# Taking four blocks' second 128 columns as they lie, in a sparse graph kernel with row gathers

## The chip, the cores and the metric

The kernel runs on one core of one Trainium2 chip. The time is the device time in microseconds (us) of one execution; for the kernel before it is 993.78 us, the median of 3 runs (992.75 to 998.94). The trace that is read below comes from one further execution under the hardware profiler, which took longer than the timed ones (the table below has it).

The engines are named as in the profile: PE is TensorE's matmul, PEld its weight load, DVE VectorE, ACT ScalarE, POOL GpSimd and SP SyncE, which here only issues DMAs.

## The reference: four graph layers over one sparse matrix

`x` is 2708 x 512, `adj` is 2708 x 2708 with 24,436 entries that aren't zero; they are dense in the low rows and columns and on the diagonal. Each layer adds something to `x` and normalizes the rows:

```python
# layer 0: degree-normalized sum, then a product with W
adj_hat = adj + eye;  d = 1 / sqrt(adj_hat.sum(1))
x = layernorm(x + (d[:, None] * adj_hat * d[None, :]) @ x @ W.T + b)
# layer 1: every positive entry raised by its row's share, divided by the degree
head = (adj > 0) / max(norm of the row, eps);  inc = adj + head
x = layernorm(x + (inc @ x) / inc.sum(1))
# layer 2: attention weights e on the entries; h = x @ W_sa
s = s_left[:, None] + s_right[None, :]
e = where(adj != 0, exp(-leaky_relu(s, 0.01)), 0);  x_a = (e / e.sum(1)) @ h
x_b = adj @ (x @ W_gcnb) + b_gcnb
x = layernorm(x + sigmoid(gate_a * x_a + gate_b * x_b))   # gates from adj @ x and x
# layer 3: product of signs, summed over the neighbours
x = layernorm(x + relu(adj @ (max(sign(x), 0) @ sign(weight).T)))
```

## The kernel before

The 2708 rows are 22 blocks of 128 (the last has 20). For one block of rows only some columns of `adj` hold anything. The kernel finds them on the chip and packs them: a *tile* is 128 such columns (as rows of `adj_t`, 128 x 128 in SBUF, in `packed[b]`), and the rows of the features that belong to them are fetched by an indirect DMA, a *gather* of 128 rows whose addresses stand in `index[b]`. A block's sum is then a chain of matmuls, one per tile, into one PSUM bank. The packed tiles and the indices are made once and used by all four layers.

`ROOM[b]` is how many gathered tiles block `b` has. `DIRECT[b]` names column blocks that are not searched: they are taken as they lie, 128 x 128 of `adj_t` by a plain DMA on SP's queue (line 1000), and their features are a block already in SBUF, so that they need no gather. Before, only block 1 has more than column block 0. Block 0 itself takes all 22 column blocks directly. `HALVES[b]` is (tiles whose columns only reach the upper 64 rows of the block, tiles for the lower 64 rows); a half tile has 64 columns of weights, and an upper and a lower one can share the PE array. `in_turns` sets the order: whole tiles, direct ones first, then upper and lower in turns.

The stages:

- *Search and layer 0's product* (lines 678 to 1268). SP streams `adj` row block by row block in the order of `arrival` (block 0 last). `mark` (line 806) clears the direct columns' part of a mask (line 845) and counts hits by matmuls; `count`, `steps_of`, `look_up` (ACT copies the table, line 931) and `list_nodes` (line 966) turn them into indices, for the groups of blocks in `GROUPS` at once. `list_nodes` also issues the direct tiles' loads. `fetch` (line 1012) then gathers the group's packed tiles from `adj_t` on POOL. After every second of these gathers POOL writes zeros into a scratch tile nobody reads (line 1020), but only for the groups in `RESTED`: all but the last three, that is up to blocks 12 to 14. In between, `y = x @ W` of each block is made, scaled and stored to DRAM (`y_rows`). The instructions of this stage are kept in the written order on each engine (`in_order`).
- *Layer 0* (from line 1319) takes the blocks in the order 1, 21, 2, 3, ..., 20. `gathered` (line 582) gathers rows of `y_rows` on POOL into a ring of 10 tiles. The positive entries are counted for layer 1, and block 0's layer 1 sum grows block by block (`grow1`).
- *Layer 1* (from line 1513) gathers from `x1_rows` into a ring of 8, makes its weights on DVE in runs of up to three tiles of one kind (lines 1601, 1602), and projects each finished block for layer 2 (line 1537).
- *Layer 2* (from line 1629) gathers rows of x and h together (1026 columns) into a ring of 7 (line 1725), makes the attention weights in parts of up to three tiles on ACT and DVE, and multiplies each tile twice (line 1748).
- *Layer 3* (from line 1916) gathers 16-bit rows of `xw_rows` for blocks 21 and 5 to 20, while the sums of blocks 0 to 4 run over all columns (`whole_tile`). Halves aren't used here.

A gather runs on POOL, in order with everything else there; its data land later through the DMA engines. If the found columns don't fit `ROOM` and `HALVES`, a flag (`over`) starts a dense version of the whole computation behind the sparse one.

Of the kernel before, what the change touches and what calls it, by code (L numbers as in the profile page):

```python
# [27 lines left out]

ROOM = (0, 8, 8, 7, 6, 6, 6, 5, 5, 5, 5, 4, 5, 4, 4, 4, 4, 4, 4, 4, 3, 1)


DIRECT = {1: (0, 1), 2: (0,), 3: (0,), 4: (0,), 5: (0,), 7: (0,), 8: (0,), 9: (0,), 11: (0,),
          13: (0,), 14: (0,), 15: (0,), 16: (0,), 17: (0,), 20: (0,)}

HALVES = ((0, 0), (3, 3), (3, 3), (2, 3), (2, 2), (2, 3), (2, 2), (2, 2), (2, 2), (2, 2), (2, 2),
          (1, 1), (2, 2), (1, 1), (1, 1), (1, 2), (1, 2), (1, 2), (1, 1), (1, 2), (1, 1), (0, 0))  # L40
HALF = 64

GROUPS = (
# [452 lines left out]
def sparse_layers(ctx, tc, x, adj, adj_t, w0_t, b0, w_sa, a_sa, w_gcnb, b_gcnb, wa, ba, wb, bb, w3_t,  # L496
# [33 lines left out]

    f = [feat.tile([P, D], F32, tag=f"f{b}", name=f"f{b}") for b in range(NB)]
    f0_other = feat.tile([P, D], F32, tag="f0_other", name="f0_other")
    first = [f[0], f0_other]
    packed = [feat.tile([P, NB, P], F32, tag="a0", name="a0")] + [
        feat.tile([P, tiles(b), rows(b)], F32, tag=f"a{b}", name=f"a{b}") for b in range(1, NB)
    ]
# [39 lines left out]
    head0_row = const.tile([P, P], F32, name="s_head0_row")  # L576
    cols = const.tile([P, NB, EXTRA], F32, name="s_cols")

    def own_by_itself(b: int) -> bool:
# [89 lines left out]
    with tc.tile_pool(name="s_pre", bufs=1) as pre:  # L669
# [10 lines left out]
        row_sums = pre.tile([P, NB, 2], F32, name="s_row_sums")  # L680

        def place_of_x(b: int):
            return f[b] if b else first[1]

        def load(b: int):
            m = rows(b)
# [119 lines left out]
        def mark(b: int, others):  # L806

            others = iter(others)  # L810

            def other():
                next(others, lambda: None)()

            g = group_of[b]
            i = g.index(b)
            m = rows(b)
            if i == 0:
                find = ps_s.tile([P, D], F32, tag="find", name=f"find{b}", bufs=2)
                n = len(g)  # L820
                search[g] = {
                    "hits": find[:, : n * NB * 3].rearrange("p (g s c) -> p g s c", g=n, c=3),
                    "before": find[:, n * NB * 3 : n * (NB * 3 + 3)],
                    "diff": find[:, D - n * NT * 4 :],
                }
            mask = masks[arrival.index(b) % 2]
            for ar, c0 in zip(arows[b], (0, CUT)):
                nc.vector.tensor_scalar(
                    mask[:m, c0 : c0 + ar.shape[1]], ar, 0.0, None, op0=ALU.not_equal
                )  # L830
                other()
                own = b * P - c0
                if own_by_itself(b) and 0 <= own < ar.shape[1]:
                    nc.vector.scalar_tensor_tensor(
                        mask[:m, b * P : b * P + m], ar[:, own : own + m], 0.0, off_dia[:m, :m],
                        op0=ALU.not_equal, op1=ALU.mult,
                    )
                    other()
                    scr = small.tile([P, P], F32, tag="dia", name=f"dia{b}", bufs=1)
                    nc.vector.scalar_tensor_tensor(  # L840
                        scr[:m, :m], ar[:, own : own + m], 1.0, ident[:m, :m],
                        op0=ALU.mult, op1=ALU.mult, accum_out=dia[:m, b : b + 1],
                    )
            for j in direct(b):
                nc.vector.memset(mask[:m, j * P : (j + 1) * P], 0.0)
            for step_ in others:
                step_()
            for s in range(NB):
                nc.tensor.matmul(
                    search[g]["hits"][:, i, s, :], mask[:m, s * P : (s + 1) * P], sides[:m],  # L850
                    start=True, stop=True,
                )
# [152 lines left out]
                at += ROOM[b]  # L1005

        to_fetch = []
        RESTED = GROUPS[:-3]
        fetched = [0]
        rest = pre.tile([P, 384], F32, name="s_rest")  # L1010

# [102 lines left out]
        def head_steps(g):  # L1114
# [41 lines left out]

            def keep_heads():
                hr = counts_of.pop(g)
                dst = head0_row if g == (0,) else head_row[:, b0_ * P : b0_ * P + G * m]
                nc.scalar.copy(dst, hr[:, : G * m])  # L1160

            return [counts, roots, shares, spread, keep_heads]

        counts0 = small.tile([P, 2], F32, tag="counts", name="counts0", bufs=1)

        def count_block0():
# [111 lines left out]
    bw = wp.tile([P, KC, D], BF16, name="s_bw")  # L1278
    sequence = [0, 1, NB - 1, *range(2, NB - 1)]

    def features(b: int, i: int, old0):

        j = direct(b)[i]
        return f[j] if j else old0


    def span(b: int, i: int):
# [39 lines left out]
    with tc.tile_pool(name="s_l0", bufs=10, reuse_waits="tile") as lp:  # L1327


        a_row = lp.tile([P, 2, D], F32, tag="a_row", name="s_a_row", bufs=1)  # L1330
        vec = lp.tile([P, 2, KC], F32, tag="vec", name="s_vec", bufs=1)
        b0_row = lp.tile([P, D], F32, tag="b0_row", name="s_b0_row", bufs=1)
        nc.scalar.dma_start(b0_row, over_partitions(b0, D))

# [31 lines left out]
        def grow1(j: int):  # L1366

            r = rows(j)
            inc = lp.tile([P, P], F32, tag="inc0", name=f"inc0_{j}", bufs=2)
            a = packed[0][:r, j, :]  # L1370
            nc.vector.scalar_tensor_tensor(
                inc[:r], a, 0.0, head0_row[:r], op0=ALU.is_gt, op1=ALU.mult
            )
            nc.vector.tensor_tensor(inc[:r], inc[:r], a, op=ALU.add)
            nc.tensor.matmul(  # L1375
                sum1, inc[:r], (f[j] if j else first[1])[:r, :D], start=(not grown1),
                stop=(len(grown1) == NB - 1),
            )
            grown1.append(j)
# [17 lines left out]
        for n, g in enumerate(GROUPS):  # L1397
            steps_ = head_steps(g)
            between.setdefault(2 + 2 * n, []).append(
                several(lambda g=g: count_positive(g, lp), steps_[0])  # L1400
            )
            between.setdefault(3 + 2 * n, []).append(several(*steps_[1:]))
        for at, b in enumerate(sequence):
            m = rows(b)
            old = place_of_x(b)
            nc.vector.tensor_tensor(old[:m, :D], old[:m, :D], b0_row[:m], op=ALU.add)
            if b:
                nd = len(direct(b))
                order_ = in_turns(b)
                src = {}  # L1410
                for i in order_:
                    if i >= nd:
                        src[i] = gathered(lp, D, y_rows, b, i - nd)
                    elif direct(b)[i] == b:
                        src[i] = lp.tile([P, D], F32, tag="own", name=f"y_own{b}", bufs=1)
                        nc.sync.dma_start(src[i][:m], y_rows[b * P : b * P + m, :])
                    else:
                        src[i] = first[0]
                ps = ps_mm.tile([P, D], F32, tag="mm", name=f"l0_{b}")
                for i in order_:  # L1420
# [12 lines left out]
            for step_ in between.get(at, []):  # L1433
                step_()
# [27 lines left out]
    state = {}  # L1462

    def old_new(b: int):
        return (f[b], f[b]) if b else (first[0], first[1])

    def open_block(b: int, pool, ps_pool, tag: str):

# [30 lines left out]

    def finish1(b: int, ps):  # L1500
        m = rows(b)
        old, new = (f[b], f[b]) if b else (first[1], first[0])
        t = work.tile([P, D], F32, tag="t", name=f"t1_{b}")
        nc.scalar.activation(t[:m], old[:m, :D], AF.Copy, scale=own1[:m, b : b + 1])
        nc.vector.scalar_tensor_tensor(
# [5 lines left out]
    with tc.tile_pool(name="s_l1", bufs=8, reuse_waits="tile") as lp:  # L1511
# [407 lines left out]
    with tc.tile_pool(name="s_l3", bufs=11, reuse_waits="tile") as lp, \  # L1919
# [13 lines left out]

        turn = [0]

        def widened(t, r: int, name: str):

            g = lp.tile([P, D], F32R, tag="wide", name=f"w{name}", bufs=4)
            turn[0] += 1
            if turn[0] % 3 == 0:  # L1940
                nc.vector.tensor_copy(g[:r], t[:r])
# [6 lines left out]
        def finish3(b: int, ps, more: bool):  # L1948

            m = rows(b)  # L1950
            old = f[b] if b else first[1]
# [35 lines left out]

        whole = [ps_w.tile([P, D], F32, tag=f"w{b}", name=f"l3_{b}") for b in range(WHOLE3)]

        def whole_tile(j: int):  # L1990
# [21 lines left out]
        for at, b in enumerate(order3):  # L2012
# [121 lines left out]
```

## Time and profile before

| What | us |
|---|---|
| median of 3 runs (lowest, highest) | 993.78 (992.75, 998.94) |
| the profiled execution | 1049.87 |
| its span, first to last instruction | 1048.1 |
| PE busy | 884.9 |
| DVE busy | 660.3 |
| POOL busy | 524.8 |
| first gather of layer 0 | 199.0 |
| first gather of layer 1 | 368.8 |
| first gather of layer 2 | 602.8 |
| first matmul group of layer 3 | about 917 |

In the lines of the profile, "L1014" is a line of the kernel, "out<-in" are the names of tiles, and "x12" is a count. Times in the timeline and in the chain of waits count from the span's start. In a timeline the first number is the start, the second how long the instruction (or the merged row of instructions) took, and the bracket at the end is how long the engine stood idle before it and what ended that: "issue" and "remote" or "another core or an unknown queue" mean that the profile sees nothing that ended it. DMA_INDIRECT is a gather[...].

### The profile page before, as it was taken

The numbers are of one execution on the slowest core, as the hardware profiler recorded it, in microseconds if no ns is written. First come the engines' busy times: TensorE is split into PE (matmuls) and PEld (weight loads), VectorE is DVE, ScalarE is ACT, GpSimd is POOL, SyncE is SP. The second block draws the span as 40 slices with busy tenths as digits, with TensorE's granted clock in tenths as the row PEclk, the third lists the DMA queues.
The fourth block names the chain that finished last, engine by engine and source line by source line (L and its number), as shares of the span: only waits on it lengthen the run. The fifth ranks groups of instructions, "written<-read, shape, count | busy, mean of one in ns | idle before, by whom it ended". The sixth has DMA issues, their size and how long they took to land.

```text
span 1048.1 us, 13071 instructions
## 1 busy us (share of the span) xinstructions
PE 884.9 (84%) x3759; PEld 467.4 (45%) x3777; DVE 660.3 (63%) x2598; ACT 385.7 (37%) x824; POOL 524.8 (50%) x555
## 2 busy tenths in 40 slices
PE   1999885567879959999999989988788999689993
PEld 1545442122223224545555533444444555467862
DVE  4889795545657745554654456666577777655675
ACT  3665562000000114534444433333333333255553
POOL 1688885766766254644532053343243333066761
PEclk9999997778989988999999999999899999889996
DMA  9999982667767454766554266776566665299985
GB/s 285 345 348 329 314 279 62 204 177 213 221 207 214 144 177 142 220 187 188 178 176 129 102 229 217 260 243 203 173 223 208 202 192 181 80 280 315 328 240 174
DMA packets 94759, 225.07 MB, mean 215 GB/s; under 512 B 13900, under 2 KB 28092, under 8 KB 94676
## 3 DMA queue, kind: packets, MB, share of 16 engines
q0 software_dynamic: 44784, 132.86, 42.7%
q1 hardware_dynamic: 37944, 76.51, 21.3%
q10 hardware_dynamic: 11948, 14.76, 4.4%
q8 instruction: 32, 0.52, 0.2%
q14 instruction: 51, 0.42, 0.1%
HBM read 182.80 MB, written 31.71 MB: 205 GB/s over the span
## 4 chain that ended last, share of the span: by engine, by line
PE 58%; DVE 12%; DMA 12%; issue 6%; another core or an unknown queue 4%; ACT 4%; POOL 3%; ACTq 0%; POOLq 0%; DVEq 0%; SPq 0%
PE l L1320 16%; DMA xg<-x_rows,i 9%; PE h L1537 7%; PE l L2003 5%; PE a L1748 4%; PE e L1748 4%; PE l L2042 3%; PE pg L1800 3%; PE y L1048 2%; PE pc L1800 2%; POOL a L1014 2%; PE l L1375 2%; PE e L1570 2%; PE a L1571 1%
## 5 line engine op out<-in xcount | busy, mean ns | idle before, releaser
L1725 POOL DMA_INDIRECT xg<-x_rows,i x102 | 100.3, 984 | 180.3 <-PE e L1748 45.2
L584 POOL DMA_INDIRECT xg<-x_rows,i x102 | 98.0, 961 | 117.5 <-PE l L1320 74.2
L1014 POOL DMA_INDIRECT a<-in_adj_t_dram,row_at x102 | 112.2, 1100 | 61.9 <-DVE deg L773 26.5
L584 POOL DMA_INDIRECT xg<-y_rows,i x102 | 103.1, 1010 | 48.3 <-issue 23.5
L1320 PE MATMUL l<-xg,a 128*64 128x512 f32 (+2 forms) x204 | 91.4, 684 | 12.4 <-DMA xg<-y_rows,i 12.4
L1748 PE MATMUL a<-xg,a 128*64 128x512 f32 (+2 forms) x204 | 91.4, 602 | 4.7 <-DMA xg<-x_rows,i 4.7
L584 POOL DMA_INDIRECT xg<-xw_rows,i x73 | 74.3, 1018 | 40.8 <-issue 18.6
L1748 PE MATMUL e<-xg,ae 128*64 128x512 f32 (+2 forms) x204 | 89.3, 602 | 1.4 <-ACT ae L1498 1.4
L1048 PE MATMUL y<-s_w,xt 128*128 128x512 f32 (+1 forms) x176 | 87.4, 642 | 1.6 <-issue 0.9
L1537 PE MATMUL h<-s_wsa,xt 128*128 128x256 f32 (+3 forms) x352 | 83.8, 392 | 3.0 <-issue 1.9
L1537 PEld LDWEIGHTS h<-s_wsa,xt 128*128 128x128 f32 (+1 forms) x352 | 65.7, 190 | 29.0 <-issue 10.7
L1320 PE MATMUL l<-xg,inc 128*64 128x512 f32 (+2 forms) x204 | 73.4, 609 | 2.5 <-DMA xg<-x_rows,i 2.3
L1493 ACT ACTIVATE ae<-sl,xg 128x64 f32<-128x64 f32 (+2 forms) x102 | 35.8, 359 | 84.8 <-DMA xg<-x_rows,i 76.0
L765 ACT ACTIVATE unused<-arow 128x1408 uint8<-128x1408 f32 (+3 forms) x44 | 58.3, 1325 | 3.6 <-DMA x_rows<-s_zero 2.0
L613 ACT ACTIVATE rsqs<-mv 128x1 f32<-128x1 f32 (+2 forms) x56 | 11.3, 202 | 126.2 <-DVE mv L642 42.8
L2003 PE MATMUL l<-ws,pw 128*128 128x512 f32 (+1 forms) x210 | 51.3, 398 | 4.8 <-DVE pw L1931 4.8
L1800 PE MATMUL pg<-s_wg,pt 128*128 128x256 f32 (+1 forms) x176 | 46.0, 403 | 8.2 <-ACT pt L1788 8.2
L1048 PEld LDWEIGHTS y<-s_w,xt 128*128 128x128 f32 (+1 forms) x176 | 33.2, 199 | 39.6 <-issue 38.0
L1494 DVE SCALAR_TENSOR_TENSOR ae<-ae 128x128 f32<-128x128 f32 (+4 forms) x60 | 19.9, 334 | 47.8 <-ACT ae L1493 41.9
L1544 DVE COPY h<-h 128x260 f32<-128x260 f32 (+1 forms) x20 | 8.6, 428 | 64.9 <-PE h L1537 41.6
L1320 PEld LDWEIGHTS l<-xg,a 128*64 128x64 f32 (+2 forms) x204 | 23.7, 167 | 55.9 <-issue 51.8
L2003 PEld LDWEIGHTS l<-ws,pw 128*128 128x128 f32 (+1 forms) x210 | 39.7, 190 | 14.8 <-DVE pw L1931 5.6
(302 smaller groups left out, 1854.0 us busy)
## 6 DMA issues: line engine op xcount, KB each, us to landing
arow<-in_adj_dram SPq DMA_DIRECT2D x21, 704.0 KB
arow<-in_adj_dram SPq DMA_DIRECT2D x21, 650.0 KB
x_rows<-f SPq DMA_DIRECT2D x41, 256.0 KB
aw<-in_adj_t_dram SPq DMA_DIRECT2D x21, 320.0 KB
f<-in_x_dram SPq DMA_DIRECT2D x20, 256.0 KB
y_rows<-yt ACTq DMA_DIRECT2D x20, 256.0 KB
out_dram<-f SPq DMA_DIRECT2D x20, 256.0 KB
x_rows<-h SPq DMA_DIRECT2D x19, 257.0 KB
```

Source lines behind the costliest of these rows:

```text
L584: nc.gpsimd.indirect_dma_start(out=t, out_offset=None, in_=src[:, :], in_offset=bass.IndirectOffsetOnAxis(ap=index[b][:, i : i + 1], axis=0),)
L765: nc.scalar.activation(unused[:m, : ar.shape[1]], ar, AF.Copy, accum_out=row_sums[:m, b, h : h + 1])
L1014: nc.gpsimd.indirect_dma_start(out=packed[b][:, t + len(direct(b)), :], out_offset=None, in_=adj_t, in_offset=bass.IndirectOffsetOnAxis(ap ...
L1048: nc.tensor.matmul(ps[:m], xt[:, k, :m], w0[:, k, :], start=(k == 0), stop=(k == KC - 1))
L1320: nc.tensor.matmul(ps[r0:r1], weights, moving, start=(i == order[0]), stop=all(span(b, j) != (r0, r1) for j in order[order.index(i) + 1 :] ...
L1493: nc.scalar.activation(ev[:, i, :], sl, AF.Identity, bias=score)
L1537: nc.tensor.matmul(ps, xt[:, k, :m], w[:, k, :], start=(k == 0), stop=(k == KC - 1))
L1725: nc.gpsimd.indirect_dma_start(out=g, out_offset=None, in_=x2_rows[:, :], in_offset=bass.IndirectOffsetOnAxis(ap=index[b][:, t : t + 1], a ...
L1748: nc.tensor.matmul(ps[r0:r1], weights, moving, start=(i == order[0]), stop=all(span(b, k) != (r0, r1) for k in order[order.index(i) + 1 :] ...
L1800: nc.tensor.matmul(ps, pt[:, k, :m], w[:, k, :], start=(k == 0), stop=(k == KC - 1))
L2003: nc.tensor.matmul(whole[b], p[:r, h, b * P : (b + 1) * P], g[:r, :], start=(j == 0 and h == 0), stop=(j == NB - 1 and h == 1),)
L2042: nc.tensor.matmul(ps[:m], p[:, h, i * m : (i + 1) * m], src[i0 + i], start=False, stop=(i0 + i == len(src) - 1 and h == 1),)
```

## The change

Blocks 3, 5, 15 and 17 take column block 1 directly as well as column block 0. Each has one gathered tile less and one direct tile more, so that there are 98 gathers per layer instead of 102 (in layer 3, where blocks 1 to 4 gather nothing, 70 instead of 73), and as many in the search. Their `HALVES` lose one lower half tile. Because column block 1 is now read by later blocks, block 1 has two places, as block 0 had before: one with the layer's old features and one with the new (`f1_other`, `pairs`). In layer 0 the tile with block 1's own y stays for the later blocks; in layer 3 block 1's widened tile (`wide1`) stays. `RESTED` takes in one more group, blocks 15 to 17, so that the scratch fills also stand between that group's gathers in the search. To make room, a small row (`head0_row`) and a scratch tile (`dia`) move to other pools.

```diff
-ROOM = (0, 8, 8, 7, 6, 6, 6, 5, 5, 5, 5, 4, 5, 4, 4, 4, 4, 4, 4, 4, 3, 1)
+ROOM = (0, 8, 8, 6, 6, 5, 6, 5, 5, 5, 5, 4, 5, 4, 4, 3, 4, 3, 4, 4, 3, 1)
-DIRECT = {1: (0, 1), 2: (0,), 3: (0,), 4: (0,), 5: (0,), 7: (0,), 8: (0,), 9: (0,), 11: (0,),
-          13: (0,), 14: (0,), 15: (0,), 16: (0,), 17: (0,), 20: (0,)}
+DIRECT = {1: (0, 1), 2: (0,), 3: (0, 1), 4: (0,), 5: (0, 1), 7: (0,), 8: (0,), 9: (0,), 11: (0,),
+          13: (0,), 14: (0,), 15: (0, 1), 16: (0,), 17: (0, 1), 20: (0,)}
-HALVES = ((0, 0), (3, 3), (3, 3), (2, 3), (2, 2), (2, 3), (2, 2), (2, 2), (2, 2), (2, 2), (2, 2),
-          (1, 1), (2, 2), (1, 1), (1, 1), (1, 2), (1, 2), (1, 2), (1, 1), (1, 2), (1, 1), (0, 0))
+HALVES = ((0, 0), (3, 3), (3, 3), (2, 2), (2, 2), (2, 2), (2, 2), (2, 2), (2, 2), (2, 2), (2, 2),
+          (1, 1), (2, 2), (1, 1), (1, 1), (1, 1), (1, 2), (1, 1), (1, 1), (1, 2), (1, 1), (0, 0))
...
-    first = [f[0], f0_other]
+    f1_other = feat.tile([P, D], F32, tag="f1_other", name="f1_other")
+    pairs = {0: [f[0], f0_other], 1: [f[1], f1_other]}
...
-            return f[b] if b else first[1]
+            return pairs[b][1] if b in pairs else f[b]
...
-                    scr = small.tile([P, P], F32, tag="dia", name=f"dia{b}", bufs=1)
+                    scr = pre.tile([P, P], F32, tag="dia", name=f"dia{b}", bufs=1)
...
-        RESTED = GROUPS[:-3]
+        RESTED = GROUPS[:-2]
...
+        head0_row.append(lp.tile([P, P], F32, tag="head0_row", name="s_head0_row", bufs=1))
...
+        y_direct = {0: pairs[0][0]}
...
-                    elif direct(b)[i] == b:
-                        src[i] = lp.tile([P, D], F32, tag="own", name=f"y_own{b}", bufs=1)
-                        nc.sync.dma_start(src[i][:m], y_rows[b * P : b * P + m, :])
                     else:
-                        src[i] = first[0]
+                        if direct(b)[i] == b:
+                            y_direct[b] = lp.tile([P, D], F32, tag="own", name=f"y_own{b}", bufs=1)
+                            nc.sync.dma_start(y_direct[b][:m], y_rows[b * P : b * P + m, :])
+                        src[i] = y_direct[direct(b)[i]]
...
-        old, new = (f[b], f[b]) if b else (first[1], first[0])
+        new, old = pairs.get(b, (f[b], f[b]))
...
-                src = {i: features(b, i, first[1]) for i in range(nd)}
+                src = {i: place_of_x(direct(b)[i]) for i in range(nd)}
...
-                g = widened(g, r, f"s{j}")
+                g = widened(g, r, f"s{j}", "wide" if j > 1 else "wide1", 4 if j > 1 else 1)
+                if j == 1:
+                    xw_direct[1] = g
...
-            src = [xw0] * len(direct(b)) + sources3.pop(b)
+            src = [xw_direct[j] for j in direct(b)] + sources3.pop(b)
```

More of the change, by code (lines that the diff above doesn't have):

```diff
@@ L575, in sparse_layers @@
     own1 = const.tile([P, NB], F32, name="s_own1")
-    head0_row = const.tile([P, P], F32, name="s_head0_row")
     cols = const.tile([P, NB, EXTRA], F32, name="s_cols")
@@ L1158, in keep_heads @@
                 hr = counts_of.pop(g)
-                dst = head0_row if g == (0,) else head_row[:, b0_ * P : b0_ * P + G * m]
+                dst = head0_row[0] if g == (0,) else head_row[:, b0_ * P : b0_ * P + G * m]
                 nc.scalar.copy(dst, hr[:, : G * m])
             return [counts, roots, shares, spread, keep_heads]
+        head0_row = []
         counts0 = small.tile([P, 2], F32, tag="counts", name="counts0", bufs=1)
@@ L1279, in sparse_layers @@
     sequence = [0, 1, NB - 1, *range(2, NB - 1)]
-    def features(b: int, i: int, old0):
-        j = direct(b)[i]
-        return f[j] if j else old0
     def span(b: int, i: int):
@@ L1371, in grow1 @@
             nc.vector.scalar_tensor_tensor(
-                inc[:r], a, 0.0, head0_row[:r], op0=ALU.is_gt, op1=ALU.mult
+                inc[:r], a, 0.0, head0_row[0][:r], op0=ALU.is_gt, op1=ALU.mult
             )
@@ L1375, in grow1 @@
             nc.tensor.matmul(
-                sum1, inc[:r], (f[j] if j else first[1])[:r, :D], start=(not grown1),
+                sum1, inc[:r], place_of_x(j)[:r, :D], start=(not grown1),
                 stop=(len(grown1) == NB - 1),
@@ L1464, in old_new @@
     def old_new(b: int):
-        return (f[b], f[b]) if b else (first[0], first[1])
+        return tuple(pairs.get(b, (f[b], f[b])))
     def open_block(b: int, pool, ps_pool, tag: str):
@@ L1934, in sparse_layers, with widened @@
         turn = [0]
-        def widened(t, r: int, name: str):
-            g = lp.tile([P, D], F32R, tag="wide", name=f"w{name}", bufs=4)
+        def widened(t, r: int, name: str, tag: str = "wide", bufs: int = 4):
+            g = lp.tile([P, D], F32R, tag=tag, name=f"w{name}", bufs=bufs)
             turn[0] += 1
@@ L1950, in finish3 @@
             m = rows(b)
-            old = f[b] if b else first[1]
+            old = place_of_x(b)
             k = len(moments)
@@ L1988, in sparse_layers @@
         whole = [ps_w.tile([P, D], F32, tag=f"w{b}", name=f"l3_{b}") for b in range(WHOLE3)]
+        xw_direct = {0: xw0}
         def whole_tile(j: int):
```

## The prediction

> **What bounds the kernel now.** I began with the page: the engines' shares and the chain of work that ended last.
>
> ```profile
> span 1048.1 us, 13071 instructions
> PE 884.9 (84%) x3759; PEld 467.4 (45%) x3777; DVE 660.3 (63%) x2598; ACT 385.7 (37%) x824; POOL 524.8 (50%) x555
> PE 58%; DVE 12%; DMA 12%; issue 6%; another core or an unknown queue 4%; ACT 4%; POOL 3%; ACTq 0%; POOLq 0%; DVEq 0%; SPq 0%
> ```
>
> TensorE (PE) is the bound on average, but a tenth of the chain is "issue" or "unknown queue": waiting for nothing the profile can name. So I asked for busy time by stretch. The search runs to 199 us, layer 0 to about 371, layer 1 to 606, layer 2 to 917, layer 3 to the end.
>
> ```profile
> core 0: us, PE busy (x) PEld busy (x) DVE busy (x) ACT busy (x) POOL busy (x), PEclk, DMA share, GB/s
> 120.00:160.00 40.00, 36.55 (x274) 20.26 (x273) 34.98 (x151) 22.77 (x43) 34.09 (x38) 0.96 0.87 274
> 160.00:199.00 39.00, 21.84 (x89) 8.65 (x87) 21.77 (x102) 7.10 (x16) 23.12 (x23) 0.81 0.41 106
> 199.00:225.00 26.00, 12.04 (x31) 3.54 (x32) 6.23 (x24) 0.30 (x2) 18.61 (x19) 0.63 0.66 201
> 303.00:330.00 27.00, 27.00 (x92) 9.44 (x90) 19.73 (x89) 1.97 (x7) 19.20 (x19) 0.98 0.73 218
> 500.00:560.00 60.00, 60.00 (x215) 32.89 (x212) 32.92 (x132) 28.18 (x48) 25.32 (x27) 1.00 0.55 167
> 720.00:760.00 40.00, 33.35 (x135) 19.41 (x137) 24.97 (x100) 11.98 (x35) 12.44 (x14) 0.91 0.50 165
> 800.00:840.00 40.00, 39.06 (x162) 22.67 (x164) 32.07 (x127) 15.56 (x45) 13.23 (x15) 1.00 0.62 200
> ```
>
> PE is full from 303 us through layer 1 and late in layer 2. It is loose at the hand-over from the search to layer 0 (160 to 225) and somewhat in the first half of layer 2. The pieces of the chain around that hand-over, then POOL's and ACT's own timelines there:
>
> ```profile
> 162.93 12.79 another core or an unknown queue
> 182.48 1.40 POOL a L1014
> 199.04 1.48 POOL xg L584
> 215.21 8.47 issue
> ```
>
> ```profile
> 157.98 0.44 POOL L1020 MEMSET s_rest<- 128x384 f32 x1
> 158.58 0.95 POOL L1014 DMA_INDIRECT a<-in_adj_t_dram,row_at  x1 [0.16 <-DVE root L632]
> 159.83 0.95 POOL L1014 DMA_INDIRECT a<-in_adj_t_dram,row_at  x1 [0.30 <-issue]
> ...
> 172.33 0.94 POOL L1014 DMA_INDIRECT a<-in_adj_t_dram,row_at  x1 [0.30 <-issue]
> 182.48 1.40 POOL L1014 DMA_INDIRECT a<-in_adj_t_dram,row_at  x1 [9.21 <-DVE s_own L1065]
> ```
>
> ```profile
> 175.74 0.41 ACT L931 CAST steps<-find 128x300 bf16<-128x300 f32 x1 [12.61 <-remote]
> ```
>
> The last fill ends at 158.4. Then POOL issues the 12 gathers of blocks 15 to 17 unbroken, one per 1.25 us (0.95 busy, 0.30 idle), to 173.3. Meanwhile ACT stands for 12.6 us before the copy that the lists of blocks 18 to 20 need. Its data were ready: the matmul of line 924 ended at 164.16, but the trace has TensorE's count rising only at 175.72. So POOL waits 9.2 us for the next lists, and layer 0's first gather goes out at 199.04.
>
> **The change part by part.** Sums are against the profiled execution (1049.87 us, span 1048.1), 56.1 us above the median of the runs (993.78).
>
> *TensorE.* Each of the four blocks swaps a half-height gathered tile that had no partner (2 above and 3 below become 2 and 2; 1 and 2 become 1 and 1) for one full tile. Back to back in layer 0, full tiles take 0.86 to 0.98 us (284.93 to 285.79; two from 285.79 to 287.74), a lone half 1.01 (309.51 to 310.52), three halves of which two share the array 1.86 (288.21 to 290.07). The unpaired half thus costs what a full one does: 0 in layers 0 to 2. In layer 3 halves aren't used and the tile count stays: 0.
>
> *Search, blocks 3 and 5.* Two gathers fewer, 2.5 us of POOL. But POOL waited for VectorE's lists at 67.42 (0.67 us) and 88.57 (1.43 us), after these groups, so the gain turns into longer waits: 0 (bounds -1 and 0). From 88.57 POOL never waits again until 173.3.
>
> *Search, blocks 15 and 17, and the fills.* Two gathers fewer: -2.5. The counter stands at 76 before this group, so ten gathers carry five fills. A fill costs at least 0.44 + 0.16 - 0.30 = 0.30 us (memset, and a shorter gap behind it). Between 88.57 and 158.58 the 43 filled gathers took 70.0 us, 1.63 each; over 1.25 that is about 0.75 per fill[...]. Five are 1.5 to 3.8 us; I take 2.5, between the ends[...]. Sum 0 (bounds -1.0 and +1.3), all on POOL's path to layer 0; a fill waits for nothing, and behind it on POOL stand only gathers. [...] The fills' row shows 432 ns least, 438 median, 1086 most. [...]
>
> *The stall behind the unbroken run.* If breaking the run lets ACT's copy go at 164.2, the last lists come about 11 us sooner, and POOL's 9.2 us wait is gone. POOL itself is then next: 158.6 + 15 us, 12 more gathers, and layer 0 starts near 189 instead of 199. That is -9.2 to -11.5. [...] Two numbers decide for me. The nameless pieces over 1 us on the chain (12.8, 11.2, 8.5, 7.8, 6.2, 5.9, 5.6 and eight shorter) sum to 73 us, and the profiled execution is 56 us longer than the timed ones. They are of one size, and they stand where gathers run unbroken. I take 0 for the timed run (bounds -11.5 and 0); the trace may show it though the times don't.
>
> *Direct tiles.* Four loads of 64 KB on SP's queue replace four gathers of the same bytes. SP spends about 0.45 us on each. Behind those of blocks 3 and 5 queue the next rows of adj; at 66.40 and 86.71 such pairs took 0.9 and 1.6 us while rows were already on their way two blocks ahead: 0 (with no cover, +1.6). Those of 15 and 17 go out near 151 to 159, after all the rows. Four more mask clears at 0.11 us on VectorE: 0.
>
> *Layer 0.* Gathers cost 1.25 us of POOL each: 69 of them between 199 and 303 are 86 of 104 us, so POOL paces the first blocks. Blocks 3 and 5 lose one each: -2.5. Blocks 15 and 17 come where PE is full: 0. Bounds 0 (if PE, at 71.5 of those 104 us, is next) and -5. The tile of block 1's own y stays in its buffer: no extra wait.
>
> *Layer 1.* PE is full, gathers hidden: 0. Block 3's weights come in four runs instead of three, two more VectorE steps of 0.285 us, with VectorE about half busy: 0. Bounds -0.5 and +0.6. Block 1 now keeps old and new x apart, at no instruction.
>
> *Layer 2.* PE has 34.8 us of gaps over 0.5 us for 102 gathers, 0.34 each; four fewer are -1.4. Block 5 also has two parts instead of three. Bounds 0 (15 and 17 run at 39 of 40) and -4.5 (the gaps of 1.1, 0.8 and 2.6 us at 683, 705 and 715 closed).
>
> *Layer 3.* Three gathers fewer beside a PE at 93%: -0.3 (0 to -1).
>
> Sum: 0 - 2.5 + 0 - 1.4 - 0.3 = -4.2, all in the timed run as in the profiled one: 993.8 - 4.2 = about 989.5.
>
> **The rivals.** *The stall is real:* [...] For it: an engine waited in the trace with its input ready. Against: the 56 us. Price 9.2 to 11.5 more: about 979.
>
> *Slower:* the fills are dear. They lie on the only path to layer 0's first gather; at 1086 ns each costs 1.09 + 0.16 - 0.30 = 0.95, five 4.75 against 2.5 saved, +2.3, and PE takes layer 0's POOL gain back: 996. It decides if a fill costs over 0.5 us, nothing comes back in layers 0 and 2, and no stall is removed. For it: several fills took 1.0 to 1.1. Against: five in a row never did.
>
> *The stall moves:* it is real, and the unbroken run of the 12 last gathers and layer 0's first ones now stops PE earlier: a gain as in the likeliest case, or a loss of up to 12.
>
> That the change doesn't do what it says I could count on the inputs: blocks 3, 5, 15 and 17 need 729, 607, 372 and 360 gathered rows of 768, 640, 384 and 384. Nothing overflows, the dense path isn't taken.
>
> **How the numbers follow.** Likeliest, small savings and no stall in the timed runs, 989 (985 to 992): 0.60. Stall real and gone, 979 (976 to 983): 0.21. Fills dear or stall moved by its length, 993 to 997: 0.15. Something over 1% slower: 0.04. The range 980 to 994 leaves out half of the second case and part of the third. Within 1% (9.9 us, about what a measurement of this kernel can tell from no change) lie the first, the third and a little of the second: faster 0.20, same 0.76, slower 0.04.
>
> **What would show it.** Five fills among ten gathers from about 158; the wait before ACT's copy of line 931 short, POOL's 9.2 us wait gone, and the first layer 0 gather near 189 (a span near 1035), while the timed gain is far smaller. Layer 0 would end with fewer POOL-paced gaps before block 6, and layer 1 be as long as before. I am wrong if the timed gain nears 10 us[...], or if layer 0 lasts as long as before.

## The result, and the profile after

The changed kernel takes 985.99 us (median of 22 runs, 976.45 to 993.57) against 994.89 us for the kernel before beside it (22 runs, 992.75 to 1002.14). The ratio is 0.9907, with a 95% interval from 0.9889 to 0.9925: 9.2 us less, between 7.5 and 11.0. The prediction was 989, or some 4 to 5 us less.

The kernel before takes about 994 us in some sets of runs and about 1052 us in others, and the profile shown ahead of the prediction is of the longer kind while the times beside it are of the shorter. So each kernel is compared below only with the kernel before of its own set. The profile after (span 987.2 us, its execution 988.9) is read against a *new profile* of the kernel before (span 992.6 us, its execution 994.32); the one ahead of the prediction (span 1048.1 us) is called the *old profile*.

The page of the changed kernel: span, busy time of each engine, and the shares of the chain that ended last.

```profile
span 987.2 us, 13047 instructions
PE 876.2 (89%) x3755; PEld 467.9 (47%) x3773; DVE 663.5 (67%) x2597; ACT 387.1 (39%) x822; POOL 506.3 (51%) x540
PE 59%; DMA 19%; DVE 12%; POOL 4%; ACT 3%; issue 3%; ACTq 0%; DVEq 0%; SPq 0%; POOLq 0%
```

The same three lines of the new profile.

```profile
span 992.6 us, 13089 instructions
PE 876.6 (88%) x3777; PEld 464.7 (47%) x3777; DVE 662.9 (67%) x2598; ACT 386.7 (39%) x824; POOL 523.4 (53%) x555
PE 55%; DMA 18%; DVE 12%; POOL 6%; issue 6%; ACT 2%; ACTq 0%; POOLq 0%; SPq 0%; DVEq 0%
```

PE's busy time is the same within half a microsecond. What shrank is POOL, by 17 us, and "issue" on the chain, from 6 to 3%. The second is no saving in itself: 14 us of it (a piece of 13.98 at 320.18) is the wait before layer 1's first gather, which stands in both kernels (14.89 and 14.53 us, shown below), nameless in one and named in the other. "Another core or an unknown queue" stands in neither. The nameless waiting that the prediction spent a paragraph on is absent from the kernel before too, once it runs at 994 us.

The busy time by stretch, at the end of the search and through layer 0. First the new profile of the kernel before, then the changed kernel. The columns are those of the header.

```profile
core 0: us, PE busy (x) PEld busy (x) DVE busy (x) ACT busy (x) POOL busy (x), PEclk, DMA share, GB/s
160.00:187.00 27.00, 8.76 (x29) 3.14 (x28) 15.61 (x53) 1.74 (x7) 20.60 (x22) 0.75 0.59 158
187.00:220.00 33.00, 27.02 (x62) 7.21 (x62) 14.49 (x58) 0.87 (x4) 25.69 (x25) 0.89 0.68 194
260.00:300.00 40.00, 39.88 (x140) 13.93 (x141) 31.80 (x146) 3.48 (x13) 30.56 (x32) 1.00 0.82 250
```

```profile
160.00:187.00 27.00, 14.07 (x51) 4.76 (x50) 21.26 (x87) 3.40 (x11) 21.64 (x23) 0.80 0.58 162
187.00:220.00 33.00, 29.66 (x68) 8.23 (x68) 15.37 (x59) 0.87 (x4) 25.39 (x26) 0.90 0.72 209
260.00:300.00 40.00, 38.44 (x144) 13.78 (x143) 30.44 (x139) 3.74 (x14) 30.55 (x32) 0.96 0.80 244
```

Between 260 and 300 us PE is busy for 39.88 of 40 us, and one would call it the bound there. But look at POOL in the same row: 30.56 us in 32 instructions. Thirty-two gathers at 1.25 us each (0.95 busy, 0.30 between two) are exactly 40 us. POOL is full as well, though a quarter of its time isn't counted as busy. Its own timeline shows it. The new profile of the kernel before, at the turning points; in brackets the idle time ahead of the instruction, and what ended it.

```profile
43.18 1.42 POOL L1014 DMA_INDIRECT a<-in_adj_t_dram,row_at  x1 [5.83 <-DVE deg L773]
...
155.70 0.94 POOL L1014 DMA_INDIRECT a<-in_adj_t_dram,row_at  x1 [0.16 <-DVE s_kinds L1260]
...
186.81 0.95 POOL L584 DMA_INDIRECT xg<-y_rows,i  x1 [0.30 <-DMA a<-in_adj_t_dram,row_at]
...
319.23 0.95 POOL L584 DMA_INDIRECT xg<-y_rows,i  x1 [0.30 <-issue]
335.07 0.94 POOL L584 DMA_INDIRECT xg<-x_rows,i  x1 [14.89 <-issue]
```

In all that the dots leave out, from 43.18 to 319.23 us, no gather has more than 0.31 us of idle time ahead of it. POOL runs as one unbroken queue through the last three quarters of the search (to 186.81, the first gather of layer 0) and through layer 0's gathers. Then it waits 14.89 us for layer 1's. So it is POOL that sets the pace there, not PE and not the transfers: a POOL that ran ahead of either would have to wait for one of the ring's ten tiles. PE, for its part, does wait for gathered rows in layer 0, 27.1 us in the new profile and 18.7 in the changed kernel (the last number of each line):

```profile
L1320 PE MATMUL l<-xg,a 128*64 128x512 f32 (+2 forms) x204 | 94.5, 630 | 27.7 <-DMA xg<-y_rows,i 27.1
L1317 PE MATMUL l<-xg,a 128*64 128x512 f32 (+2 forms) x196 | 87.1, 633 | 19.0 <-DMA xg<-y_rows,i 18.7
```

POOL's timeline in the changed kernel:

```profile
42.85 1.42 POOL L1014 DMA_INDIRECT a<-in_adj_t_dram,row_at  x1 [5.88 <-DVE deg L773]
...
84.68 1.57 POOL L1014 DMA_INDIRECT a<-in_adj_t_dram,row_at  x1 [2.44 <-DVE s_own L1065]
...
157.89 0.95 POOL L1014 DMA_INDIRECT a<-in_adj_t_dram,row_at  x1 [0.30 <-issue]
158.83 0.44 POOL L1020 MEMSET s_rest<- 128x384 f32 x1
159.44 0.95 POOL L1014 DMA_INDIRECT a<-in_adj_t_dram,row_at  x1 [0.16 <-issue]
160.69 1.08 POOL L1014 DMA_INDIRECT a<-in_adj_t_dram,row_at  x1 [0.30 <-issue]
...
185.11 0.95 POOL L584 DMA_INDIRECT xg<-y_rows,i  x1 [0.30 <-issue]
...
327.94 1.18 POOL L584 DMA_INDIRECT xg<-x_rows,i  x1 [14.53 <-DVE inc L1600]
```

It has the same queue with eight gathers fewer in it, four of the search and four of layer 0. A new fill shows its price: from 157.89 to 160.69 two gathers and a fill take 2.80 us, 0.30 more than two gathers alone. One new wait of 2.44 us stands at 84.68, for VectorE's lists. ACT's copy of line 931, which had waited 12.61 us in the old profile, waits 1.28 us in the new one and 4.34 us in the changed kernel, both times for its own input. So it needs no fills to be short. The new profile, then the changed kernel:

```profile
152.83 0.41 ACT L931 CAST steps<-find 128x300 bf16<-128x300 f32 x1 [1.28 <-PE find L924]
158.36 0.41 ACT L931 CAST steps<-find 128x300 bf16<-128x300 f32 x1 [4.34 <-PE find L924]
```

The stages, from the starts of the first gathers (layer 3 from its first matmul), in us. The last column is an experiment told below.

| stage | before, new profile | after | after, second profile | after, four gathers put back in layer 0 |
|---|---|---|---|---|
| search | 186.8 | 185.1 | 183.8 | 186.7 |
| of it from the gather at about 43 us | 143.6 | 142.3 | 139.9 | 140.6 |
| layer 0 | 148.3 | 142.8 | 141.5 | 148.1 |
| layer 1 | 219.5 | 218.8 | 218.9 | 219.2 |
| layer 2 | 320.4 | 326.3 | 321.2 | 319.8 |
| layer 3 | 117.7 | 114.2 | 117.0 | 115.8 |
| span | 992.6 | 987.2 | 982.5 | 989.6 |

Layer 0 and the search hold the gain: together 7.2 us in the first profile of the changed kernel and 9.8 in the second. Layers 2 and 3 scatter by several microseconds from profile to profile, so a single record can't tell a microsecond there.

### The profile page after: what moved, and what is told of

The parts are those of the page before. It is cut to its first block, busy times and chain, and to the rows that moved or that the text cites. A ratio compares the mean times of both kernels' runs of the same rounds, so it can differ in the third digit from the quotient of the medians.

```text
span 987.2 us, 13047 instructions
## 1 busy us (share of the span) xinstructions
PE 876.2 (89%) x3755; PEld 467.9 (47%) x3773; DVE 663.5 (67%) x2597; ACT 387.1 (39%) x822; POOL 506.3 (51%) x540
## 4 chain that ended last, share of the span: by engine, by line
PE 59%; DMA 19%; DVE 12%; POOL 4%; ACT 3%; issue 3%; ACTq 0%; DVEq 0%; SPq 0%; POOLq 0%
PE l L1317 14%; DMA xg<-x_rows,i 10%; PE h L1536 8%; PE l L2006 5%; PE e L1747 5%; PE a L1747 5%; DMA xg<-y_rows,i 4%; PE l L2045 4%; PE pg L1799 3%; PE pc L1799 2%; POOL a L1014 2%; PE y L1048 2%; PE l L1373 2%; DMA arow<-in_adj_dram 2%; PE e L1569 2%
## 5 line engine op out<-in xcount | busy, mean ns | idle before, releaser
L1724 POOL DMA_INDIRECT xg<-x_rows,i x98 | 97.4, 994 | 193.2 <-PE e L1747 62.5
L584 POOL DMA_INDIRECT xg<-x_rows,i x98 | 94.1, 960 | 101.8 <-PE l L1317 65.4
L1014 POOL DMA_INDIRECT a<-in_adj_t_dram,row_at x98 | 107.0, 1092 | 51.5 <-DVE deg L773 26.1
L584 POOL DMA_INDIRECT xg<-y_rows,i x98 | 98.8, 1008 | 29.9 <-issue 14.0
L1317 PE MATMUL l<-xg,a 128*64 128x512 f32 (+2 forms) x196 | 87.1, 633 | 19.0 <-DMA xg<-y_rows,i 18.7
L584 POOL DMA_INDIRECT xg<-xw_rows,i x70 | 70.2, 1003 | 33.7 <-issue 12.3
L1536 PE MATMUL h<-s_wsa,xt 128*128 128x256 f32 (+3 forms) x352 | 81.7, 385 | 0.2
L1317 PE MATMUL l<-xg,inc 128*64 128x512 f32 (+2 forms) x196 | 68.7, 609 | 1.2 <-DMA xg<-x_rows,i 1.2
L1493 DVE SCALAR_TENSOR_TENSOR ae<-ae 128x128 f32<-128x128 f32 (+3 forms) x58 | 20.0, 346 | 51.7 <-ACT ae L1492 51.2
L828 DVE TENSOR_SCALAR s_mask<-arow 128x1408 bf16<-128x1408 f32 (+3 forms) x42 | 39.7, 946 | 9.5 <-DMA arow<-in_adj_dram 9.5
L638 DVE BATCH_NORM_STATS2 st<-t 128x6 f32<-128x512 f32 (+1 forms) x66 | 45.1, 684 | 0.2
```

The costliest lines, as they stand in the source:

```text
L584: nc.gpsimd.indirect_dma_start(out=t, out_offset=None, in_=src[:, :], in_offset=bass.IndirectOffsetOnAxis(ap=index[b][:, i : i + 1], axis=0),)
L638: nc.vector.bn_stats(st[:m], t[:m])
L828: nc.vector.tensor_scalar(mask[:m, c0 : c0 + ar.shape[1]], ar, 0.0, None, op0=ALU.not_equal)
L1014: nc.gpsimd.indirect_dma_start(out=packed[b][:, t + len(direct(b)), :], out_offset=None, in_=adj_t, in_offset=bass.IndirectOffsetOnAxis(ap ...
L1317: nc.tensor.matmul(ps[r0:r1], weights, moving, start=(i == order[0]), stop=all(span(b, j) != (r0, r1) for j in order[order.index(i) + 1 :] ...
L1536: nc.tensor.matmul(ps, xt[:, k, :m], w[:, k, :], start=(k == 0), stop=(k == KC - 1))
```

## The experiments

**Which time is the kernel's?** The old profile was 56 us over the timed runs, and the prediction put that down to the recording: its author's estimate, from 73 us of nameless pieces beside those 56. The kernel before, unchanged, was profiled again.

> The kernel before, unchanged, recorded once more. If the nameless stalls of its first trace (12.6 us of ACT at 163, 8.5 us of PE at 215, and so on, 73 us in all) belong to that one recorded execution, a second record has few of them: a span of 992 to 1000 us and layer 0's first gather near 188. If they are the kernel's (set off by unbroken gathers), they stand there again: a span of 1035 to 1050 and the first gather near 199.

It took 1046.38 us (span 1044.7), and its set's timed median was 1052.55 (43 runs). The record was no longer than the timed runs. The chain of waits has the nameless pieces again, of the same sort, some at other places:

```profile
163.31 11.32 another core or an unknown queue
201.59 17.05 another core or an unknown queue
243.19 11.91 another core or an unknown queue
379.25 11.24 another core or an unknown queue
```

In a later set the same kernel was profiled a third time.

> The kernel before, unchanged, a third record. Two theories of the nameless stalls are left after the first job, whose timed runs were as long as its traces (1052 us): that they belong to the chip or the hour the job ran on, or that recording brings them. If to the chip, this record and the timed runs beside it agree, whichever they are: both near 994 with layer 0's first gather near 188, or both near 1050. If recording brings them, the record is near 1048 while the timed runs beside it are near 994.

It took 994.32 us (span 992.6) beside a timed median of 995.74, with no nameless piece. Record and timed runs agree in both sets, and each timed run has a span and a granted clock on record as the profiled ones have, so recording can't be what tells 994 from 1052 us. What does is open. The record gives chip number 1 for both of these sets, so the number of the chip doesn't decide it.

**The fills alone**, on the kernel before, in the set where that takes 1052.55 us:

```diff
-        RESTED = GROUPS[:-3]
+        RESTED = GROUPS[:-2]
```

> The kernel before with the five (here six) added fills between the gathers of blocks 15 to 17 and nothing else; tiles and gathers as before. If the fills remove a real stall, this alone gives most of the measured gain: a ratio of 0.990 to 0.993. If no such stall is in the timed runs, six fills of 0.3 to 0.75 us lie on POOL's path to layer 0: a ratio of 1.001 to 1.004 (994.9 becomes 996 to 999).

1053.58 us, ratio 0.9999 (0.997 to 1.0028). The fills save nothing and cost nothing that shows beyond some 3 us. The chain in this kernel:

```profile
172.48 6.94 another core or an unknown queue
216.30 9.05 another core or an unknown queue
246.87 11.55 another core or an unknown queue
```

The piece behind the now broken run of gathers is shorter (6.94 us), and others of 9 and 12 us stand further on. POOL's wait for the last lists, 9.21 us in the old profile, is shorter as well, and still the time is the same:

```profile
184.86 1.40 POOL L1014 DMA_INDIRECT a<-in_adj_t_dram,row_at  x1 [6.50 <-DVE s_own L1065]
```

The same edit ran once more in another set:

> The kernel before with six added fills between the gathers of blocks 15 to 17 and nothing else, on a chip where the kernel before shows no nameless stalls. The single changes of blocks 3 and 5 (0.9966) and of 15 and 17 (0.9978), both without added fills, multiply to 0.9944; the whole change has 0.9907. If the fills pay the rest, 0.996 to 0.997 here. If they only cost their 0.30 us on POOL, 1.001 to 1.002. If they are neutral, 1.000, and the rest is the spread of the single runs.

1053.8 us, ratio 0.9992 (0.9959 to 1.0026), with pieces of 7.18, 17.29 and 11.82 us at 171.66, 205.70 and 247.70. The prediction's rival, that the fills remove a real stall and with it 9 to 11 us, is refuted where the stall exists. At 994 us, where it doesn't exist, the fills alone were not measured.

**The moved tiles alone**: the changed code with the old constants.

```diff
-ROOM = (0, 8, 8, 6, 6, 5, 6, 5, 5, 5, 5, 4, 5, 4, 4, 3, 4, 3, 4, 4, 3, 1)
+ROOM = (0, 8, 8, 7, 6, 6, 6, 5, 5, 5, 5, 4, 5, 4, 4, 4, 4, 4, 4, 4, 3, 1)
...
-        RESTED = GROUPS[:-2]
+        RESTED = GROUPS[:-3]
```

(`DIRECT` and `HALVES` go back likewise.)

> The changed kernel's code with the tiles, gathers and fills of the kernel before: block 1 has two places, the small tiles lie in other pools, but DIRECT, ROOM and HALVES are the old ones. If neither the moved tiles nor the two places matter, a ratio of 1.000 (0.998 to 1.002). If other addresses or a wait gone (a buffer written in place) are a hidden part of the gain, 0.994 to 0.997.

1052.26 us, ratio 0.9997 (0.9972 to 1.0023). The second place of block 1 and the moved row and scratch tile do nothing to the time that shows beyond some 3 us.

**The direct tiles without the new fills**: the changed kernel with

```diff
-        RESTED = GROUPS[:-2]
+        RESTED = GROUPS[:-3]
```

> The changed kernel without the added fills: column block 1 direct for blocks 3, 5, 15 and 17, fills only up to blocks 12 to 14. If the gathers saved are what pays, this keeps the whole gain and the fills' cost back: a ratio of 0.987 to 0.991. If a stall removed by the fills pays, it keeps only the 4 us of the direct tiles: a ratio of 0.995 to 0.998.

1046.98 us against 1052.55, ratio 0.9846 (0.9776 to 0.9915). The ratio rests on three of its six runs, so it is faster, of uncertain size. It was run again where the kernel before takes 995.74 us, beside the changed kernel itself.

> The changed kernel without the added fills. If the direct tiles pay and the fills cost their time on POOL, 0.988 to 0.990 where the changed kernel takes 0.991; if the fills pay, 0.994 to 0.997; if they are neutral, the same ratio as the changed kernel beside it within 0.002.

> The changed kernel, unchanged. Where the kernel before takes 994, the measured 0.991 again. Where it takes 1052: if the change's gain is only gathers, about 9 us, 0.991; if shorter unbroken runs also take away stalls, 0.94 to 0.985.

Without the new fills 986.49 us, ratio 0.99 (0.9862 to 0.9939). With them 983.97, ratio 0.9873 (0.9836 to 0.9911). The gain is that of the direct tiles. With four runs of each, an effect of the fills of a few microseconds either way can't be told.

**Two blocks at a time**, without the new fills. Blocks 3 and 5 alone, by difference from the changed kernel:

```diff
-          13: (0,), 14: (0,), 15: (0, 1), 16: (0,), 17: (0, 1), 20: (0,)}
+          13: (0,), 14: (0,), 15: (0,), 16: (0,), 17: (0,), 20: (0,)}
...
-        RESTED = GROUPS[:-2]
+        RESTED = GROUPS[:-3]
```

(`ROOM` and `HALVES` of blocks 15 and 17 go back likewise.)

> The changed kernel with column block 1 direct for blocks 3 and 5 only, no added fills. By my sum the gain comes from POOL's pace in the first blocks of layer 0 (2.5 us) and from layer 2's first half: this keeps three quarters of the gain of all four blocks. If a gather is worth the same in every block, it keeps half. If the last group's gathers in the search are what pays (2.5 us on POOL's path to layer 0), it keeps less than half.

992.75 us, ratio 0.9966 (0.9944 to 0.9987), 3.4 us less. And blocks 15 and 17 alone, the mirror of that edit:

```diff
-DIRECT = {1: (0, 1), 2: (0,), 3: (0, 1), 4: (0,), 5: (0, 1), 7: (0,), 8: (0,), 9: (0,), 11: (0,),
+DIRECT = {1: (0, 1), 2: (0,), 3: (0,), 4: (0,), 5: (0,), 7: (0,), 8: (0,), 9: (0,), 11: (0,),
...
-        RESTED = GROUPS[:-2]
+        RESTED = GROUPS[:-3]
```

> The changed kernel with column block 1 direct for blocks 15 and 17 only, no added fills. The prediction gave these blocks nothing in layer 0 (PE full there) and little in layer 2: 0 to -1.5 us without the fills' cost and -2.5 us in the search, a ratio of 0.9975. If POOL's gathers at 1.25 us pace the search's end and all of layer 0 without a break, as the second trace of the kernel before looks, two gathers are saved twice: -5.0 us, 0.995.

994.75 us, ratio 0.9978 (0.996 to 0.9995), 2.2 us less. Both pairs gain, the late one only just clear of nothing (0.5 to 4.0 us). But the 5.0 us that was expected if POOL paces the search's end and all of layer 0 lies outside that interval. Layer 0 was 143.5 us in the first pair's profile and 146.3 in the second's, against 148.3 before; the second's is 2.0 less, where two gathers are 2.6. Its layer 1 took 222.8 us against 219.5, and its span was 992.6 us, that of the kernel before. So what POOL saves in this profile didn't all reach the end, and why is open.

Multiplied, the two ratios give 0.9944, 5.6 us. Against the four blocks without the new fills (0.99, four runs) the missing 4.4 us are within the intervals taken together. Against the whole change (9.2 us) the missing 3.6 us are slightly more than those intervals allow (3.3, the root of the sum of their squares). They aren't assigned.

**The gathers put back in layer 0.** If POOL's queue is the pace of layer 0, then the changed kernel with one more gather for each of the four blocks there must lose about what it had gained. The extra gathers fill a tile that nobody reads.

```diff
                     if i >= nd:
+                        if b in (3, 5, 15, 17) and i == nd:
+                            gathered(lp, D, y_rows, b, i - nd)
                         src[i] = gathered(lp, D, y_rows, b, i - nd)
```

> The changed kernel with one more gather of y rows in layer 0 for each of blocks 3, 5, 15 and 17, into the same ring of tiles and read by nobody: POOL's work of layer 0 as before, PE's as changed. If POOL paces all of layer 0: 4 x 1.25 = 5.0 us above the changed kernel, a ratio of 0.996 where the changed kernel has 0.991. If it paces only the first blocks: 2.5 us, 0.9935. If the gain isn't POOL's time at all: 0.991.

991.26 us, ratio 0.9951 (0.992 to 0.9982): 4.4 us of the 9.2 are gone again (0.9951 less 0.9907). That is clear of nothing, but the interval holds the 0.9935 that was expected if POOL paces only the first blocks as well as the 0.996 for all of layer 0, so the times alone don't choose between the two. In the profile layer 0 takes 148.1 us, as before the change, though its matmuls are those of the changed kernel. The gathers of layer 0 in three kernels: count, ns least, median and most, and the first and last start. The changed kernel, the new profile of the kernel before, and this experiment:

```profile
L584 POOL DMA_INDIRECT xg<-y_rows,i x98: 942/946/2462, 185.1 to 312.4; - x98
```

```profile
L584 POOL DMA_INDIRECT xg<-y_rows,i x102: 942/946/2769, 186.8 to 319.2; - x102
```

```profile
L584 POOL DMA_INDIRECT xg<-y_rows,i x102: 943/949/2006, 186.7 to 321.5; - x102
```

From first to last start, 97 steps take 127.3 us and 101 steps take 132.4 us, 1.31 us each in both. The experiment has 134.7 us. One wait of 4.04 us in it stands in neither of the others:

```profile
307.62 0.94 POOL L584 DMA_INDIRECT xg<-y_rows,i  x1 [4.04 <-DMA xg<-y_rows,i]
```

Without the 3.74 us that this wait has over an ordinary gap, the stretch is 131.0 us, still 3.7 us over the changed kernel's, which is about three of the four gathers' price. So the record's layer 0 overstates the return, and the timed 4.4 us (1.3 to 7.5 by the interval of this ratio alone) are the better number. They are near 4 x 1.25 = 5.0. The extra gathers bring back their transfers too; that POOL and not the transfers makes the pace rests on POOL's timeline above.

**The gathers put back in layers 1, 2 and 3 only**, again read by nobody (for blocks 3, 5, 15 and 17 in layers 1 and 2, for 5, 15 and 17 in layer 3):

```diff
+                        if b in (3, 5, 15, 17) and i == nd:
+                            gathered(lp, D, x1_rows, b, i - nd)
...
+                        if b in (3, 5, 15, 17) and i == nd:
+                            gathered_2(b, i - nd)
...
+            if b in (5, 15, 17):
+                gathered(lp, D, xw_rows, b, 0, F32R)
```

> The changed kernel with one more gather, read by nobody, in layers 1 and 2 for each of blocks 3, 5, 15 and 17, and in layer 3 for 5, 15 and 17; layer 0 and the search as changed. If those layers hide their gathers, the changed kernel's 0.991 (0.989 to 0.993). If layer 2's four cost what the prediction gave them (1.4 us) and layer 3's 0.3, 0.9925. If layer 2's ring of 7 paces it, 3 us per gather, 12 us in all: 1.003.

1049.94 us against 1053.54, ratio 0.9974 (0.9947 to 1.0001), without the changed kernel beside it. Its span was 1055.3 us, with layer 2 at 328.9 and layer 3 at 130.7 us. This settles nothing: what the changed kernel gains in such a set was not measured. But it leaves a rival standing. The changed kernel has 0.9907 in the sets of 994 us, and the direct tiles without the fills 0.9846 beside 1052.55 us; by either, the extra gathers of layers 1 to 3 would cost 7 us or more here. Whether part of the gain comes from these layers is open.

## Why the prediction was right, and where not

The time lies in the range and within 1%, as the likeliest case had it. That 985.99 us falls inside 985 to 992 at all is in part luck: 9.2 us is twice the sum of 4.2, and two terms of that sum failed for one reason, the old profile.

*What bounds the kernel.* "PE is full from 303 us through layer 1" is true of the old profile. There POOL does wait in layer 0, sixteen times after 199 us and 17.3 us over its ordinary gaps, the late waits mostly for matmuls to free a tile:

```profile
303.43 0.95 POOL L584 DMA_INDIRECT xg<-y_rows,i  x1 [1.17 <-PE l L1320]
320.80 1.15 POOL L584 DMA_INDIRECT xg<-y_rows,i  x1 [1.62 <-PE l L1320]
332.65 0.95 POOL L584 DMA_INDIRECT xg<-y_rows,i  x1 [1.64 <-PE l L1320]
```

In the new profile PE is full from 260 to 300 us, yet POOL doesn't wait once before 319.23. Two engines were full, and the busy columns showed one of them. Layer 0's end followed POOL: layer 1's first gather goes out 15.8 us after layer 0's last (319.23 to 335.07) before the change, 15.5 us (312.4 to 327.94) after it.

*"Blocks 15 and 17 come where PE is full: 0"* is the step that failed for layer 0. By the count of POOL's queue all four gathers matter, 4 x 1.31 = 5.2 us instead of 2.5, the prediction's own bound of -5. The profile has 5.5 less (148.3 to 142.8), and putting the gathers back returned 4.4 in the timed runs. The cover was real in the record it was read from and absent from the kernel that was timed, whose POOL issues at 1.25 us per gather without a wait. At about 1050 us, too, layer 0 shrank by more than 2.5: in the two profiles of that length with all four direct tiles (without the new fills, and with the gathers put back behind layer 0) layer 0 took 159.8 and 162.0 us, in the five with the old tiles 169.7 to 173.1. That is more than POOL's count, and it isn't explained.

*"Search, blocks 3 and 5: 0"* failed in part. In the old profile POOL waited for lists at 67.42 and 88.57 us, and the gain was to go into longer waits. In the new one there are no such waits after 43 us, so the two gathers and the fill that falls away with them are 2 x 1.25 + 0.30 = 2.8 us of POOL's queue. The mechanism named is real all the same: the changed kernel shows one new wait, 2.44 us at 84.68 (2.14 over the ordinary gap), and another profile of it 0.43 us at the same place. In the profile of blocks 3 and 5 alone next to nothing of the 2.8 us shows (the table below).

*"Search, blocks 15 and 17, and the fills"*: the lower bound was right, not the value taken. Each of the five fills costs 0.30 us, not 0.5. The 0.75 of the whole stretch had put POOL's slow gathers on the fills' account: in that stretch of the old profile, 23 of the gathers took over 1.0 us, 7.9 us over 0.95 each in all. Ten gathers and five fills are 10 x 1.25 + 5 x 0.30 = 14.0 us where twelve gathers were 15.0: a gain of 1.0. The timeline has 14.2 us (153.86 to 168.07) against 16.0 (155.70 to 171.72), of which slow gathers are 0.3 and 1.0.

With these sizes POOL's queue from 43 us to the end of layer 0 comes to -2.8 and -1.0 in the search, -5.2 in layer 0, and up to +2.1 for the new wait. That is 6.9 to 9.0 us less, against a measured 9.2 (7.5 to 11.0). The sum was made after the result and doesn't prove itself: the same count gives 5.3 us for blocks 3 and 5 alone, where 3.4 (1.3 to 5.6) were measured, and 5.1 for 15 and 17, where 2.2 (0.5 to 4.0) were, and no timed run took the search's gathers alone. Shown by a timed run is the share of layer 0. The search alone, from the gather at 43 us, can be set against the profiles:

| kernel | gathers, fills on POOL from 43 us | its wait over 0.30 us | worked out from 143.6 | in the profile |
|---|---|---|---|---|
| before | 94, 35 | 0 | (start) | 143.6 |
| blocks 3 and 5 alone | 92, 34 | 0.1 | 140.9 | 143.5 |
| blocks 15 and 17 alone | 92, 35 | 0 | 141.1 | 142.1 |
| both, without the new fills | 90, 34 | 2.1 | 140.4 | 140.2 |
| after | 90, 39 | 2.1 | 141.9 | 142.3 |
| after, second profile | 90, 39 | 0.1 | 139.9 | 139.9 |
| after, gathers back in layer 0 | 90, 39 | 0 | 139.8 | 140.6 |

Each gather is 1.25 and each fill 0.30 us. All but one row agree within 1 us. In the row that is 2.6 us off, the fills took 20.1 us for 34, about 2 us more than the kernel before's 18.5 for 35 when counted per fill. Dear fills do occur, then, more in one profile than in the next.

*The stall.* Taking 0 for it in the timed runs was right, and the reasoning was wrong. The signs that were named for it in the trace came, but the kernel before shows them as well once it takes 994 us: a short wait before the copy of line 931 (1.28 us), no wait on POOL, and layer 0's first gather at 186.8 us against 185.1 after the change. So they say nothing of the fills. That the recording made the 56 us was an estimate, and no trace showed it. The runs show record and timed run agreeing at both lengths (1046.4 beside 1052.6, 994.3 beside 995.7), so the recording is not what made this difference. The prediction's own sign of error, a gain near 10 us, came about where there was no stall to remove.

*The rest.* Layer 1 at 0 is right (219.5 to 218.8). Layer 2's -1.4 doesn't show (320.4 to 326.3 and 321.2), though the gathers put back in layers 1 to 3 leave that open, and layer 3's -0.3 is below what a record can tell. The direct loads and the moved tiles at 0 fit the runs (0.9997 for the tiles). The slower rival needed fills at over 0.5 us and nothing back in layer 0, and neither held.

## What to carry to other kernels

When a profile's span and the timed median differ by several per cent, find a profile at the timed length before any wait, or any cover, in it is costed: here the old profile showed POOL waiting for PE where the timed kernel doesn't. Then, before a saving is counted at nothing because one engine is full, read the timeline of the engine that loses work. If it issues without a wait, as POOL did here at 0.95 us busy in every 1.25, it is full at 76% busy, and each instruction saved shortens its queue by the full interval. Price one small instruction between others from two neighbouring intervals (2.80 against 2.50 us), not from a stretch that holds slow neighbours too.

## What the runs showed of the hardware that was not expected

The same kernel has two lengths, about 994 and 1052 us. In the old profile the search takes 199.0 us instead of the new one's 186.8, layer 0 169.7 instead of 148.3, layer 1 234.1 instead of 219.5 and layer 3 126.9 instead of 117.7, while layer 2, at 318.4 against 320.4, is no longer. The chain then has pieces of 7 to 17 us in which an engine waits for nothing that the profile names. At 163 us in the old profile TensorE's count rose 11.6 us after the matmul of line 924 had ended by the profile (164.16 to 175.72). By these two times alone, a matmul that ended late and a count that rose late can't be told apart. Fills between the gathers didn't remove these pieces.

The granted clock is lower too, 0.941 and 0.946 in the two records of the kernel before at that length against 0.962 in the new one, but it doesn't start the standstill. Where PE stops, at about 165 us in the old profile, the clock is still at 0.93, and 0.50 comes after it (the column PEclk, third from the end):

```profile
core 0: us, PE busy (x) PEld busy (x) DVE busy (x) ACT busy (x) POOL busy (x), PEclk, DMA share, GB/s
164.00:168.00 4.00, 1.30 (x13) 1.13 (x11) 1.93 (x10) 0.00 (x0) 3.09 (x4) 0.93 0.35 63
168.00:172.00 4.00, 0.00 (x0) 0.00 (x0) 0.00 (x0) 0.00 (x0) 3.08 (x4) 0.50 0.24 50
```

PE's busy time over the whole span is 8.3 us longer (884.9 against 876.6), a small part of the 56. Neither the cause of the pieces nor what decides the length was found.
